# Attention with a group norm on one core: normalisation spread over steps, projections moved later, x loaded first, the last sums inverted from PSUM

## The chip, the cores and the metric

The kernel runs on one core of a Trainium2 chip. The metric is device time in microseconds (us) of one execution; the profile's span is the time from the first to the last instruction of one profiled execution. A core has five engines with a queue of instructions each: PE (matrix multiply; PEld is its weight load), DVE (vector), ACT (scalar, activation functions), POOL (GpSimd) and SP, which here only issues DMAs. PE writes to PSUM, a memory of eight banks; ACT and DVE copy from there to SBUF.

## The reference

```python
def reference(x, q_w, q_b, kv_w, kv_b):        # x: 32 images, 256 channels, 32 x 32 positions
    return x + attention(group_norm(x))

def group_norm(v, G=32, eps=1e-5):             # 32 groups of 8 channels, over 8 * 1024 values
    return (v - mean) / sqrt(var + eps)

def attention(xf):                             # S = 1024 positions, 8 heads of 32 channels
    q = q_w @ xf + q_b;  k, v = split(kv_w @ xf + kv_b)
    scores = q.T @ k / sqrt(32)
    scores = where(position of key < position of query, scores, -10000)
    attn = softmax(scores)
    attn = where(position of key < position of query, attn, 0)
    return attn @ v
```

All is float32. The first query sees no key, so its output is x alone.

## The kernel before

**Tiles and steps.** Channels lie on partitions, 256 channels are two groups `g` of 128, which are four heads each. The 1024 queries are two halves `hf` of 512 columns, the keys eight blocks `k` of 128. One *step* is one block of keys for four heads and one half of the queries. Since a query sees only earlier keys, half 0 has the blocks k = 0 to 2 and half 1 the blocks 0 to 6 (the fourth block of a half is done together with its second, in `blocks`), so an image has 2 x (3 + 7) = 20 steps (`N`): steps 0 to 2 are (g 0, half 0), 3 to 9 (g 0, half 1), 10 to 12 (g 1, half 0), 13 to 19 (g 1, half 1). With 32 images there are 640 steps.

**One step.** `scores` multiplies k by q into two PSUM tiles `sT` (tag sT has three buffers of two banks each), and ACT writes exp of each into the SBUF tile `e`. On the last blocks of a half POOL clears the entries of later keys (`affine_select`). Two steps later (`LAG = 2`) `values` multiplies `e` by v into `acc`, and DVE adds `e` to the running total. The total is no tile of its own: it is the `e` tile of the half's first block, k = 0, which has the tag `e0` and **two buffers**. The others have the tag `e` and four.

**The end of a half.** `values` of the last block ends with an ACT copy of `acc` to `num`. `sums` then lets PE add the total over partitions (`pd`, from `e` and the ones in `pick`), ACT copies `pd` to `den`, and a DMA writes it to DRAM. When an image's four halves are there, `gather` reads them back as 128 rows of 64, `invert` checks their range and takes the reciprocal on DVE (`inv`), and more DMAs bring the inverses back, spread over partitions, as `rb`. `finish` multiplies `num` by `rb`, adds the v bias and x, and stores it.

**Before an image's steps.** `load` brings x by DMA. `norm_channels` takes the statistics of each channel (DVE, `mv`), `norm_mean` averages them over a group on PE (`pm`), copies that with ACT (`mean`) and at once lets DVE work out `dev` from it; `norm_rstd` averages dev on PE (`pv`), adds eps on ACT and takes the power -0.5 on POOL; `norm_apply` writes `xn` on DVE. `projections` are 12 units of PE work: eight `project_qk` (`pp`) and four `project_v` (`ppv`), each ended by an ACT copy out of PSUM.

**PSUM.** sT takes six banks, acc one, and a single bank, the tag `misc`, serves pm, pv, pp, ppv and pd in turn: each has to be copied out before the next may start.

**Who sets the order.** PE, ACT, DVE and POOL run their instructions in the order in which the program is written (`manual_schedule`); SP's is chosen by the framework. The loop at the end goes over the steps: at step i it writes `scores` of step i, then the work that the table `at` has for i, then `values` of step i - 2, then what the table `after` has. Before the change, the statistics of image b + 2 stand at steps 4 and 5 of image b, mean at 8, rstd at 10, apply at 16 and 18; the projections of image b + 1 at 12 steps of image b; the sums of a half at the third step after its last (so at steps 5, 12, 15 and 2 of the next image). Images 0 and 1 are normalised and image 0 is projected ahead of the loop.

Of the kernel before, what the change touches and what calls it, by code (L numbers as in the profile page):

```python
# [9 lines left out]
F32 = mybir.dt.float32  # L10
# [7 lines left out]
P = 128  # L18
# [13 lines left out]
def tile_norm_attention_residual(  # L32
# [59 lines left out]


    wT = const.tile([P, NG, 3 * C], F32, name="wT")
    with tc.tile_pool(name="wload", bufs=3) as wload, tc.tile_pool(name="ps_w", bufs=2, space=PSUM) as ps_w:
        for n, w in enumerate((q_w, kv_w[0:C], kv_w[C : 2 * C])):
            wn = wload.tile([P, NG, C], F32, tag="wn", name=f"wn_{n}")
            nc.sync.dma_start(out=wn, in_=w.rearrange("(o p) c -> p o c", p=P))
            for cc in range(NG):
                pt = ps_w.tile([P, C], F32, tag="pt", name=f"wt_{n}_{cc}")  # L100
                for o in range(NG):
                    nc.tensor.transpose(pt[:, o * P : (o + 1) * P], wn[:, o, cc * P : (cc + 1) * P], ident)
                nc.vector.tensor_copy(wT[:, cc, n * C : (n + 1) * C], pt)
    qk_bias = const.tile([P, 2, NG], F32, name="qk_bias")
    nc.sync.dma_start(out=qk_bias[:, 0, :], in_=q_b.rearrange("(g p) -> p g", p=P))
    nc.sync.dma_start(out=qk_bias[:, 1, :], in_=kv_b[0:C].rearrange("(g p) -> p g", p=P))
    nc.vector.tensor_scalar_mul(qk_bias[:, 0, :], qk_bias[:, 0, :], SCALE)
    v_bias_col = const.tile([P, NG], F32, name="v_bias_col")
    nc.sync.dma_start(out=v_bias_col, in_=kv_b[C : 2 * C].rearrange("(g p) -> p g", p=P))
    v_bias = const.tile([P, C], F32, name="v_bias")  # L110
    nc.sync.dma_start(out=v_bias, in_=kv_b[C : 2 * C].rearrange("(o c) -> o c", o=1).broadcast_to([P, C]))

    def unshifted():
        xpool = tc.alloc_tile_pool(name="xpool", bufs=4)
        work = tc.alloc_tile_pool(name="work", bufs=2)
# [8 lines left out]
        live = {}  # L124
# [13 lines left out]

        def load(b):
            live["x", b] = xpool.tile([P, NG, S], F32, tag="x", name=f"x_{b}")  # L140
            nc.sync.dma_start(out=live["x", b], in_=x_in[b])
# [9 lines left out]
        def norm_mean(b):  # L151
# [4 lines left out]
            nc.scalar.copy(mean, pm[:, :NG])  # L156

# [4 lines left out]
            live["mean", b], live["dev", b] = mean, dev  # L162

        def norm_rstd(b):
            pv = misc(f"pv_{b}")
            product(pv[:, :NG], avg, live.pop(("dev", b)))
            rstd = small.tile([P, NG], F32, tag="rstd", name=f"rstd_{b}")
            nc.scalar.activation(rstd, pv[:, :NG], AF.Identity, bias=eps)
            nc.gpsimd.tensor_tensor(rstd, rstd, power, ALU.pow)
            live["rstd", b] = rstd  # L170

        def norm_apply(b, g):
            if g == 0:
                live["xn", b] = work.tile([P, NG, S], F32, tag="xn", name=f"xn_{b}")
            mean, rstd = live["mean", b], live["rstd", b]
            nc.vector.tensor_scalar(
                live["xn", b][:, g, :], live["x", b][:, g, :],
                mean[:, g : g + 1], rstd[:, g : g + 1], ALU.subtract, ALU.mult,
            )
# [100 lines left out]
        def sums(b, g, hf):  # L280
# [10 lines left out]
            nc.scalar.copy(den, pd)  # L291
            if n == 0:
# [6 lines left out]
        def gather(b):  # L299
# [243 lines left out]
```

## Time and profile before

| | |
|---|---|
| median of 3 runs | 2262.64 us (2260.61 to 2266.06) |
| the profiled execution's own time, and its span | 2263.33 us, 2261.6 us |
| PE busy | 2081.9 us, 92% of the span |
| DVE busy | 1514.2 us, 67% |
| ACT busy | 1492.0 us, 66% |
| POOL busy | 419.3 us, 19% |
| mean granted clock of PE, as a share of the full one | 0.970 |
| DMA | 108.01 MB, 48 GB/s in the mean |

Matmuls are pipelined, so that a row's duration overlaps the next row's by some 0.07 us or more; the time that one costs is best read from its start to the next start. An idle time in square brackets in a timeline is that of the engine ahead of the row, with what ended it.

### The profile page before, as it was taken

To read this page: it belongs to the slowest core of one execution; us is meant where nothing else is said; L and a number is where in the kernel's file an instruction comes from. 1 tells how busy PE (TensorE), PEld (TensorE's weight loads), DVE (VectorE), ACT (ScalarE), POOL (GpSimd) and SP (SyncE) were. 2 spreads that over 40 slices of the span, in tenths; PEclk is the share of its full clock that TensorE was granted. 3 is DMA by queue.
4 is the path that set the end of the run, shared out by engine and by line. 5 is a ranking of instruction groups with operands and counts; after the bars stand their busy time and mean duration, and the time that the engine had idled before them with its cause. 6 is when DMAs were issued, how large, how long until landed. Compare 5 with 4: busy or idle time off the path is not lost.

```text
span 2261.6 us, 50192 instructions
## 1 busy us (share of the span) xinstructions
PE 2081.9 (92%) x22030; PEld 733.3 (32%) x22030; DVE 1514.2 (67%) x1417; ACT 1492.0 (66%) x1985; POOL 419.3 (19%) x494
## 2 busy tenths in 40 slices
PE   4999999999999999999999999999999999999993
PEld 1333333333333333333333333333333333333331
DVE  2566767666767666776667676667676667766675
ACT  1767666667666676666676666676666766666773
POOL 0221121121121211211211212211212112112121
PEclk9999999999999999999999999999999999999997
DMA  2001111101111011111011111011110111110011
GB/s 91 2 31 50 50 48 59 56 24 59 43 55 59 31 50 58 41 58 59 30 51 49 49 59 50 30 59 43 55 59 34 46 56 42 58 59 31 31 40 59
DMA packets 47057, 108.01 MB, mean 48 GB/s; under 512 B 12656, under 2 KB 13552, under 8 KB 46832
## 3 DMA queue, kind: packets, MB, share of 16 engines
q1 hardware_dynamic: 46832, 104.74, 13.0%
q8 instruction: 174, 2.85, 0.5%
q14 instruction: 51, 0.42, 0.1%
HBM read 69.08 MB, written 35.65 MB: 46 GB/s over the span
## 4 chain that ended last, share of the span: by engine, by line
PE 73%; DVE 19%; ACT 4%; issue 3%; DMA 1%; POOL 1%; SPq 0%; DVEq 0%; POOLq 0%; ACTq 0%
PE sT L237 23%; PE pp L134 21%; PE acc L268 17%; DVE e L273 12%; PE ppv L134 6%; PE pd L286 6%; DVE rb L326 2%; ACT e L244 2%; DVE dev L159 1%; DVE rb L327 1%; DVE dev L160 1%; ACT num L277 1%; ACT q L193 1%; POOL e L250 1%; DMA rb<-inverses 0%
## 5 line engine op out<-in xcount | busy, mean ns | idle before, releaser
L273 DVE TENSOR_TENSOR e<-e,e 128x2048 f32<-128x2048 f32 (+3 forms) x640 | 1088.6, 1701 | 492.1 <-PE acc L268 192.0
L244 ACT ACTIVATE e<-sT 128x1024 f32<-128x1024 f32 (+1 forms) x1280 | 1127.8, 940 | 433.1 <-PE sT L237 424.9
L237 PE MATMUL sT<-q,k 32*128 32x512 f32 (+3 forms) x6144 | 721.2, 541 | 0.5 <-ACT e L244 0.5
L250 POOL TENSOR_SCALAR_AFFINE_SELECT e<-e 128x512 f32<-128x512 f32 (+1 forms) x384 | 351.0, 926 | 1781.9 <-ACT e L244 1042.2
L268 PE MATMUL acc<-e,v 128*32 128x512 f32 (+3 forms) x6144 | 617.4, 489 | 20.9 <-ACT num L277 11.7
L134 PE MATMUL pp<-xn,wT 128*32 128x512 f32 x4096 | 494.1, 600 | 5.9 <-ACT q L193 3.2
L237 PEld LDWEIGHTS sT<-q,k 32*128 32x128 f32 x6144 | 291.2, 187 | 433.8 <-issue 371.5
L268 PEld LDWEIGHTS acc<-e,v 128*32 128x32 f32 x6144 | 173.6, 110 | 349.5 <-issue 231.0
L134 PE MATMUL ppv<-wT,xn 128*32 128x256 f32 x4096 | 257.9, 394 | 10.9 <-ACT mean L156 8.0
L286 PE MATMUL pd<-e,pick 128*32 128x512 f32 x1024 | 150.1, 657 | 92.2 <-DVE e L273 92.2
L134 PEld LDWEIGHTS pp<-xn,wT 128*32 128x32 f32 x4096 | 107.0, 109 | 321.7 <-issue 234.8
L291 ACT COPY den<-pd 128x512 f32<-128x512 f32 x128 | 75.2, 588 | 184.4 <-PE pd L286 184.4
L134 PEld LDWEIGHTS ppv<-wT,xn 128*32 128x32 f32 x4096 | 122.9, 113 | 168.5 <-issue 68.8
L159 DVE TENSOR_TENSOR dev<-mv,mean 128x2 f32<-128x2 f32 x32 | 33.1, 1035 | 203.0 <-ACT mean L156 203.0
L326 DVE TENSOR_TENSOR rb<-num,rb 128x512 f32<-128x512 f32 x128 | 114.6, 896 | 9.8 <-DMA rb<-inverses 9.8
L193 ACT ACTIVATE k<-pp,qk_bias 128x512 f32<-128x512 f32 x128 | 88.1, 688 | 32.4 <-PE pp L134 32.4
L209 ACT COPY v<-ppv 128x512 f32<-128x512 f32 x128 | 75.1, 587 | 51.2 <-PE ppv L134 50.7
L327 DVE SCALAR_TENSOR_TENSOR rb<-rb,v_bias_col,x 128x512 f32<-128x512 f32 x128 | 105.4, 824 | 4.6
L193 ACT ACTIVATE q<-pp,qk_bias 128x512 f32<-128x512 f32 x128 | 88.1, 688 | 13.4 <-PE pp L134 9.8
L286 PEld LDWEIGHTS pd<-e,pick 128*32 128x32 f32 x1024 | 32.1, 112 | 176.6 <-DVE e L273 121.1
L148 DVE BATCH_NORM_STATS2 st<-x 128x6 f32<-128x512 f32 x128 | 80.1, 668 | 4.8 <-DMA x<-in_x_dram 4.8
L277 ACT COPY num<-acc 128x512 f32<-128x512 f32 x128 | 74.5, 582 | 3.7 <-PE acc L268 3.7
(39 smaller groups left out, 250.6 us busy)
## 6 DMA issues: line engine op xcount, KB each, us to landing
x<-in_x_dram SPq DMA_DIRECT2D x32, 1024.0 KB
rb<-inverses SPq DMA_DIRECT2D x128, 256.0 KB
out_dram<-rb SPq DMA_DIRECT2D x64, 512.0 KB
sums<-den SPq DMA_DIRECT2D x128, 8.0 KB
rows<-sums SPq DMA_DIRECT2D x32, 32.0 KB
inverses<-inv SPq DMA_DIRECT2D x32, 32.0 KB
wn<-in_L_conv_kv_w_dram SPq DMA_DIRECT2D x2, 256.0 KB
wn<-in_L_conv_q_w_dram SPq DMA_DIRECT2D x1, 256.0 KB
```

Source lines behind the costliest of these rows:

```text
L134: nc.tensor.matmul(out[part], lhsT=lhsT[:, part], rhs=rhs, start=start, stop=stop, skip_group_check=True)
L148: nc.vector.bn_stats(st[:, c, :], live["x", b][:, g, c * HALF : (c + 1) * HALF])
L193: nc.scalar.activation(live[key][:, cols], pp, AF.Identity, bias=qk_bias[:, n, g : g + 1], scale=(SCALE, 1.0)[n],)
L237: nc.tensor.matmul(pairs[j // 2][:, j % 2, cols], lhsT=kk[rows, kb * P : (kb + 1) * P], rhs=q[rows, hf * HALF + of.start : hf * HALF + of. ...
L244: nc.scalar.activation(e[:, 2 * a : 2 * a + 2, c0:], pairs[a][:, :, c0:], AF.Exp)
L250: nc.gpsimd.affine_select(out=diagonal, in_=diagonal, pattern=[[0, 4], [0, n], [1, P]], compare_op=ALU.is_gt, fill=0.0, base=0, channel_mu ...
L268: nc.tensor.matmul(acc[HD * j : HD * (j + 1), of], lhsT=live["v", b][:, kb, h * HD : (h + 1) * HD], rhs=e[:, j, cols], start=k == 0, stop= ...
L273: nc.vector.tensor_add(total[:, :, of], total[:, :, of], e[:, :, cols])
L277: nc.scalar.copy(live["num", b][:, g, hf * HALF : (hf + 1) * HALF], acc)
L286: nc.tensor.matmul(pd[HD * j : HD * (j + 1), :], lhsT=pick, rhs=total[:, j, :], start=True, stop=True, skip_group_check=True,)
L326: nc.vector.tensor_mul(rb[:, g, cols], num[:, g, cols], rb[:, g, cols])
L327: nc.vector.scalar_tensor_tensor(rb[:, g, cols], rb[:, g, cols], v_bias_col[:, g : g + 1], xt[:, g, cols], ALU.add, ALU.add)
```

## The change

Weights are loaded through ACT's queue, after the first two images' x, which now comes in two DMAs an image; ACT instead of DVE copies the transposed weights. The normalisation of an image is cut into eight functions, which stand at steps of their own: `dev` two steps after `mean`, `pv` eight steps after that, the power one step on and all of `xn` one more step on, in four pieces. The projections of an image stand from six steps before its first step to its step 11, ordered by the step that needs them; of image 0 two units are left ahead of the loop. The sums stand one step later (`SUMS = LAG + 2`), gather and invert at steps 4 and 6 of the next image, and `finish` stores each half by itself. The last image gathers three halves early, and its fourth is inverted by DVE directly from `pd` in two pieces. Nothing is added to or taken from what is computed.

```diff
+    def load_weights():
+            for wn, w in zip(wns, (q_w, kv_w[0:C], kv_w[C : 2 * C])):
+                nc.scalar.dma_start(out=wn, in_=w.rearrange("(o p) c -> p o c", p=P))
...
+                    nc.scalar.copy(wT[:, cc, n * C : (n + 1) * C], pt)
...
+        def load(b):
+            live["x", b] = xpool.tile([P, NG, S], F32, tag="x", name=f"x_{b}")
+            for g in range(NG):
+                nc.sync.dma_start(out=live["x", b][:, g, :], in_=x_in[b, :, g, :])
+
+        for b in range(min(2, B)):
+            load(b)
+        load_weights()
...
             nc.scalar.copy(mean, pm[:, :NG])
+            live["mean", b] = mean
+
+        def norm_deviation(b):
+            mv, mean = live["mv", b], live["mean", b]
...
-        def norm_rstd(b):
+            live["dev", b] = dev
+
+        def norm_variance(b):
             pv = misc(f"pv_{b}")
...
-            units = [lambda hf=hf, n=n: project_qk(b, 0, n, hf) for n in range(2) for hf in range(NH)]
-            units += [lambda n=n: project_v(b, n) for n in range(NB // 2)]
-            units += [lambda hf=hf, n=n: project_qk(b, 1, n, hf) for n in range(2) for hf in range(NH)]
-            return units
+            qk = [[lambda g=g, hf=hf, n=n: project_qk(b, g, n, hf) for n in range(2)] for g in range(NG) for hf in range(NH)]
+            v = [lambda n=n: project_v(b, n) for n in range(NB // 2)]
+            return qk[0] + v[:1] + qk[1] + v[1:3] + qk[2] + v[3:] + qk[3]
...
+        def finish_last(b):
+            g, hf = NG - 1, NH - 1
+            for c in range(2):
+                within = slice(c * HALF // 2, (c + 1) * HALF // 2)
+                nc.vector.reciprocal(
+                    live["rb", b][:, g, hf * HALF + within.start : hf * HALF + within.stop], live["pd", b][:, within]
+                )
+                finish(b, 3, within)
...
-                    when(b * N + s + LAG + 1, lambda b=b, g=g, hf=hf: sums(b, g, hf), after)
...
+        PROJECT = (-6, -5, -3, -2, -1, 1, 4, 5, 7, 8, 9, 11)
+        PREPARE = (-36, -35, -30, -28, -20, -19, -18, -18)
+        SUMS = LAG + 2
+        FINISH = (N + 11, N + 12, N + 14, N + 15)
```

**The sums on PE.** In the names, sT_1_1_0_2 is image 1, group 1, half 0, block 2, pd_1_1 the sums of image 1's second half, and the last number only counts tiles. PE's order at steps 11 to 13, before:

```order
L268 MATMUL acc_1_0_1_1073<-e_1_0_1_6_1175,v_1_550 32x256 x4
L237 MATMUL sT_1_1_0_2_0_1279<-q_1_1_773,k_1_1_848 128x256 x2
L237 MATMUL sT_1_1_0_2_1_1280<-q_1_1_773,k_1_1_848 128x256 x2
L268 MATMUL acc_1_1_0_1291<-e0_1_1_0_0_1208,v_1_550 32x512 x4
L286 MATMUL pd_1_1_1296<-e0_1_0_1_0_986,pick_67 32x512 x4
L237 MATMUL sT_1_1_1_0_0_1305<-q_1_1_773,k_1_1_848 128x512 x2
L237 MATMUL sT_1_1_1_0_1_1306<-q_1_1_773,k_1_1_848 128x512 x2
L134 MATMUL ppv_2_3_1313<-wT_77,xn_2_821 32x256 x16
```

and the same place now:

```order
L283 MATMUL acc_1_0_1_991<-e_1_0_1_6_1093,v_1_731 32x256 x4
L252 MATMUL sT_1_1_0_2_0_1181<-q_1_1_976,k_1_1_1040 128x256 x2
L252 MATMUL sT_1_1_0_2_1_1182<-q_1_1_976,k_1_1_1040 128x256 x2
L283 MATMUL acc_1_1_0_1197<-e0_1_1_0_0_1118,v_1_731 32x512 x4
L252 MATMUL sT_1_1_1_0_0_1203<-q_1_1_976,k_1_1_1040 128x512 x2
L252 MATMUL sT_1_1_1_0_1_1204<-q_1_1_976,k_1_1_1040 128x512 x2
L283 MATMUL acc_1_1_0_1197<-e_1_1_0_1_1146,v_1_731 32x384 x4
L283 MATMUL acc_1_1_0_1197<-e_1_1_0_1_1146,v_1_731 32x128 x4
L301 MATMUL pd_1_1_1221<-e0_1_0_1_0_899,pick_67 32x512 x4
L252 MATMUL sT_1_1_1_1_0_1230<-q_1_1_976,k_1_1_1040 128x512 x2
L252 MATMUL sT_1_1_1_1_1_1231<-q_1_1_976,k_1_1_1040 128x512 x2
L146 MATMUL pp_2_0_0_0_1243<-xn_2_889,wT_77 32x512 x8
```

The sums pd_1_1, which read the tile e0_1_0_1_0 of step 3, have moved from ahead of step 13's scores sT_1_1_1_0 to behind them.

**The exponentials on ACT.** ACT's order at steps 12 to 14, with the engines that each instruction waits for, before:

```order
L244 ACTIVATE e_1_1_0_2_1278<-sT_1_1_0_2_0_1279 128x2x256 [waits DVE_49,PE_49]
L244 ACTIVATE e_1_1_0_2_1278<-sT_1_1_0_2_1_1280 128x2x256 [waits PE_49]
L291 COPY den_1_1_1301<-pd_1_1_1296 128x512 [waits DMAHW6_49,PE_49]
L244 ACTIVATE e0_1_1_1_0_1304<-sT_1_1_1_0_0_1305 128x1024 [waits DVE_49,PE_49]
L244 ACTIVATE e0_1_1_1_0_1304<-sT_1_1_1_0_1_1306 128x1024 [waits PE_49]
L209 COPY v_2_1121<-ppv_2_3_1313 128x512 [waits PE_49]
```

and now:

```order
L259 ACTIVATE e_1_1_0_2_1180<-sT_1_1_0_2_0_1181 128x2x256 [waits DVE_49,PE_49]
L259 ACTIVATE e_1_1_0_2_1180<-sT_1_1_0_2_1_1182 128x2x256 [waits PE_49]
L259 ACTIVATE e0_1_1_1_0_1202<-sT_1_1_1_0_0_1203 128x1024 [waits DVE_49,PE_49]
L259 ACTIVATE e0_1_1_1_0_1202<-sT_1_1_1_0_1_1204 128x1024
L306 COPY den_1_1_1226<-pd_1_1_1221 128x512 [waits DMAHW2_49]
L259 ACTIVATE e_1_1_1_1_1229<-sT_1_1_1_1_0_1230 128x1024 [waits PE_49,Pool_49]
```

The copy of pd to den has moved behind the exponentials of step 13 and has lost its wait for PE, as has the second exponential: what they need of PE has already been waited for by the instruction ahead of them.

**The deviation on DVE.** DVE's order around `dev`, before (between two of the additions of a half 1):

```order
L273 TENSOR_TENSOR e0_2_0_1_0_1569<-e0_2_0_1_0_1569,e_2_0_1_2_1632 128x2048 [waits DVE_49,Activation_49]
L159 TENSOR_TENSOR dev_4_1749<-mv_4_1609,mean_4_1747 128x2 [waits Activation_49]
L160 TENSOR_TENSOR dev_4_1749<-dev_4_1749 128x2 [waits DVE_49]
L161 TENSOR_TENSOR dev_4_1749<-dev_4_1749,mv_4_1609 128x2 [waits DVE_49]
L273 TENSOR_TENSOR e0_2_0_1_0_1569<-e0_2_0_1_0_1569,e_2_0_1_3_1670 128x2048
```

and now:

```order
L288 TENSOR_TENSOR e0_1_0_1_0_899<-e0_1_0_1_0_899,e_1_0_1_6_1093 128x4x256 [waits Pool_49]
L346 TENSOR_TENSOR rb_0_1011<-num_0_389,rb_0_1011 128x512 [waits DMAHW6_49]
L347 SCALAR_TENSOR_TENSOR rb_0_1011<-rb_0_1011,v_bias_col_79,x_0_84 128x512 [waits DVE_49]
L171 TENSOR_TENSOR dev_3_1193<-mv_3_955,mean_3_1134 128x2 [waits Activation_49]
L172 TENSOR_TENSOR dev_3_1193<-dev_3_1193 128x2 [waits DVE_49]
L173 TENSOR_TENSOR dev_3_1193<-dev_3_1193,mv_3_955 128x2 [waits DVE_49]
```

The three operations of dev now stand behind the last addition of the half (block 6), and not between those of its blocks 2 and 3.

## Rows read from the trace of the kernel before

**Rows 1.** Who waited for whom: total us, times, longest.
```profile
DVE dev L159 <- ACT mean L156: 203.0, 32, 6.7
PE pd L286 <- DVE e L273: 92.2, 32, 3.4
```

**Rows 2.** Timeline of DVE at steps 8 to 11: start us, us, what.
```profile
975.35 1.09 DVE L159 TENSOR_TENSOR dev<-mv,mean 128x2 f32<-128x2 f32 x1 [6.74 <-ACT mean L156]
...
977.19 7.55 DVE L273 TENSOR_TENSOR e<-e,e 128x2048 f32<-128x2048 f32 x4
```

**Rows 3.** Timeline of PE at step 12 of two images: start us, us.
```profile
916.12 1.07 PE L268 MATMUL acc<-e,v 128*32 128x512 f32 x8 [0.21 <-POOL rstd L169]
920.19 1.71 PE L286 MATMUL pd<-e,pick 128*32 128x512 f32 x8 [3.00 <-DVE e L273]
921.84 2.09 PE L237 MATMUL sT<-q,k 32*128 32x512 f32 x8
...
984.63 1.06 PE L268 MATMUL acc<-e,v 128*32 128x512 f32 x8 [0.21 <-POOL rstd L169]
```

**Rows 4.** Busy time by stretch: PE, PEld, DVE, ACT, POOL, PEclk, DMA, GB/s.
```profile
920.00:922.00 2.00, 1.81 (x12) 0.32 (x12) 1.96 (x4) 0.05 (x1) 0.00 (x0) 0.62 0.00 0
922.00:924.00 2.00, 2.00 (x12) 0.50 (x16) 1.97 (x3) 0.58 (x2) 0.00 (x0) 0.53 0.67 266
...
2228.00:2232.00 4.00, 1.50 (x24) 0.64 (x24) 3.59 (x3) 0.59 (x1) 0.87 (x2) 1.00 0.00 0
```

**Rows 5.** Timeline at steps 15 and 16, sums without a wait: start us, us.
```profile
862.50 1.06 PE L268 MATMUL acc<-e,v 128*32 128x512 f32 x8
862.66 1.94 ACT L244 ACTIVATE e<-sT 128x1024 f32<-128x1024 f32 x2 [0.36 <-PE sT L237]
...
863.38 1.04 PE L286 MATMUL pd<-e,pick 128*32 128x512 f32 x8
...
864.36 1.14 PE L237 MATMUL sT<-q,k 32*128 32x512 f32 x8
864.49 0.59 ACT L291 COPY den<-pd 128x512 f32<-128x512 f32 x1
...
865.43 1.92 PE L134 MATMUL pp<-xn,wT 128*32 128x512 f32 x16
```

**Rows 6.** Timeline from the start to the first scores: start us, us.
```profile
8.99 2.29 SPq L141 DMA_DIRECT2D x<-in_x_dram  x4
14.18 1.29 DVE L148 BATCH_NORM_STATS2 st<-x 128x6 f32<-128x512 f32 x2 [4.76 <-DMA x<-in_x_dram]
...
19.98 1.53 DVE L176 TENSOR_SCALAR xn<-x,mean,rstd 128x1024 f32<-128x1024 f32 x2 [1.64 <-POOL rstd L169]
...
26.38 3.50 PE L134 MATMUL pp<-xn,wT 128*32 128x512 f32 x16 [0.37 <-ACT rstd L168]
...
29.95 0.69 ACT L193 ACTIVATE q<-pp,qk_bias 128x512 f32<-128x512 f32 x1 [3.63 <-PE pp L134]
30.69 1.92 PE L134 MATMUL pp<-xn,wT 128*32 128x512 f32 x16 [0.82 <-ACT q L193]
...
59.49 1.77 PE L237 MATMUL sT<-q,k 32*128 32x512 f32 x12
```

**Rows 7.** Timeline of the last half image: start us, us.
```profile
2200.31 1.14 PE L237 MATMUL sT<-q,k 32*128 32x512 f32 x8
...
2232.59 1.06 PE L286 MATMUL pd<-e,pick 128*32 128x512 f32 x8 [2.79 <-DVE e L273]
...
2237.97 0.22 DVE L305 SCALAR_TENSOR_TENSOR in_range<-rows,in_range 128x64 f32<-128x64 f32 x1 [5.43 <-DMA rows<-sums]
...
2238.37 0.54 DVE L308 RECIPROCAL inv<-rows 128x64 f32<-128x64 f32 x1
...
2245.20 0.69 DVE L326 TENSOR_TENSOR rb<-num,rb 128x512 f32<-128x512 f32 x1 [6.29 <-DMA rb<-inverses]
...
2254.25 0.75 DVE L327 SCALAR_TENSOR_TENSOR rb<-rb,v_bias_col,x 128x512 f32<-128x512 f32 x1
```

More of the change, by code (lines that the diff above doesn't have):

```diff
@@ L94, in tile_norm_attention_residual @@
     wT = const.tile([P, NG, 3 * C], F32, name="wT")
[L95 to L103, printed above, removed]
@@ L309, in invert @@
             live["inv", b] = dram.tile([4, 4, HALF], F32, tag="inv", name=f"inverses_{b}")
-            nc.sync.dma_start(out=spread_rows(live["inv", b]), in_=inv)
-        def spread(b):
-            rb = work.tile([P, NG, S], F32, tag="rb", name=f"rb_{b}")
-            for n in range(4):
+            nc.sync.dma_start(out=spread_rows(live["inv", b])[part], in_=inv[part])
+            live["rb", b] = work.tile([P, NG, S], F32, tag="rb", name=f"rb_{b}")
+            for n in ns:
                 g, hf = divmod(n, NH)
@@ L368, in unshifted @@
         with tc.manual_schedule(engines={ENG.PE, ENG.Activation, ENG.DVE, ENG.Pool}):
-            for b in range(min(2, B)):
-                load(b)
-                for f in prepare(b):
-                    f()
-            for f in projections(0):
-                f()
-            for i in range(max(max(at), len(steps) + LAG) + 1):
+            prepare(0, [None] * 8)
+            for n, f in zip((None, None, 0, 0, 1, 1) + PROJECT[6:], projections(0)):
+                if n is None:
+                    f()
+                else:
+                    when(n, f)
@@ new lines, in unshifted @@
+            if B > 1:
+                prepare(1, (None, None, 2, 4, 6, 7, 8, 9))
+            for b in range(B):
+                first, last = b * N, b == B - 1
+                if b >= 1:
+                    for n, f in zip(PROJECT, projections(b)):
+                        when(first + n, f)
+                if b >= 2:
+                    when(max(first - 2 * N - 2, 0), lambda b=b: load(b))
+                    prepare(b, [first + n for n in PREPARE])
+                for s, (g, hf, k) in enumerate(per):
+                    if k == hf * BPH + 2:
+                        n = first + s + (LAG if last and s == N - 1 else SUMS)
+                        when(n, lambda b=b, g=g, hf=hf: sums(b, g, hf), after)
+                if not last:
+                    when(first + N + 4, lambda b=b: gather(b, every))
+                    when(first + N + 6, lambda b=b: check_sums(b, every))
+                    when(first + N + 6, lambda b=b: invert(b, every))
+                    for n in every:
+                        when(first + FINISH[n], lambda b=b, n=n: finish(b, n))
+                else:
+                    when(first + N - 4, lambda b=b: gather(b, every[:3]), after)
+                    when(first + N - 2, lambda b=b: check_sums(b, every[:3]))
+                    when(first + N - 2, lambda b=b: invert(b, every[:3]))
+                    for n in every[:3]:
+                        when(first + N + n - 1, lambda b=b, n=n: finish(b, n))
+                    when(first + N + LAG, lambda b=b: gather(b, every[3:]))
+                    when(first + N + LAG, lambda b=b: finish_last(b))
+                    when(first + N + LAG, lambda b=b: check_sums(b, every[3:]))
@@ L376, in unshifted @@
+            for i in range(max(max(at), max(after), len(steps) + LAG) + 1):
                 if i < len(steps):
```

104 lines of the change are left out of this document (52 added, 52 removed).

## The prediction

> **What bounds the kernel now.** The granted clock and the busy shares come first: PE is busy 92% of the span, no other engine over 67%, and PE's clock averages 0.970. So the place to look is PE's remaining idle time, and the list of waits names it: 92.2 us of PE waiting for DVE ahead of `pd`, 32 times [rows 1]. The list has 203.0 us of DVE waiting for ACT's `mean` as well [rows 1], which alone would cost nothing, since DVE has time to spare; what ties the two together is the order. On DVE's timeline at steps 8 to 11 the reader sees `dev` wait 6.74 us for the mean, and behind it four additions of 7.55 us in one piece that had been ready meanwhile [rows 2]. DVE comes to the end of the half late, and `pd` needs the half's last addition.
>
> The price is in PE's timeline. At step 12 `pd` starts 4.07 us behind the start of `acc` (916.12 to 920.19) [rows 3]; where nothing holds it, it is 0.88 us (862.50 to 863.38) [rows 5]. That is 3.19 us of waiting. After it PE runs slowly: `pd` takes 1.65 us to the next start against 0.98, and the scores 2.09 against 1.14 [rows 3, 5], 1.62 us in all. The stretch shows why: the granted clock is 0.62 and then 0.53 just there [rows 4], so 1.2 GHz instead of 2.4 for some 2 us. An image lasts 68.51 us (916.12 to 984.63) [rows 3], 4.81 of them this stall. Of the 92.2 us [rows 1], 30 times 3.0 are 90, so it happens in the 30 images 1 to 30 alike.
>
> **What goes.** `dev` now stands behind the half's last addition, two steps after `mean`, and the sums one step later. Ahead of the addition that `pd` needs, DVE then has only `finish` of one half at step 11. It reaches that addition some 4 us before PE reaches `pd`, worked out from steps of 1.7 to 3.8 us. I take the whole 4.81 us as gone. The copy of the mean, the power and the smaller waits (0.21 us at each step 12 [rows 3]) stay as they are or trade places.
>
> **What comes in its stead.** The moved sums collide with a buffer. The total of a half is the `e0` tile of its first block, of which there are two. The total of step 3 is freed by `pd` of step 13, but step 13's own exponentials write the same buffer. Before, that `pd` stood ahead of the step's scores; now it stands behind them, and ACT's first exponential has to wait for it (the order shows it by the copy of `pd`, which needs no wait for PE any more). At step 3 of each image it is the same with the last half of the image before. At steps 0 and 10 the buffer has been free for four steps.
>
> The price, from the end of `pd`: the exponentials start 0.07 us later, take 1.83 us together up to the next ACT row (862.66 to 864.49), then the copy `den` takes 0.59 us, and PE goes on 0.05 us after such a copy [rows 5, 6]. That is 2.54 us to the next projection, which needs the bank `misc` empty. Without the wait PE would be there after the next scores, 1.07 us (864.36 to 865.43) [rows 5]. PE thus loses 1.47 us, twice an image, 2.94 us. This wait isn't in the trace of before, so it has bounds: nothing, if the buffer is free after all (a rival below), and about 2.0 us if the next scores, whose second tile waits for the first exponential to empty a PSUM buffer, run half of their 1.07 us late. I take 1.47: that second tile can start as soon as one of the two exponentials is through, about a microsecond before it is missed. What ACT has lost it regains in the next three steps, where it has some 3 us of work in steps of 3.4 to 3.8.
>
> An image then takes 68.51 - 4.81 + 2.94 = 66.64 us, 1.87 less; 30 of them give **-56.1 us**.
>
> **The start.** Before, SP issues x behind the weights at 8.99, the statistics begin at 14.18, `xn` at 19.98, the first projection at 26.38 behind the second image's normalisation, and the first scores at 59.49 [rows 6]. Now x is issued at about 1 us; with its 5.2 us to landing (8.99 to 14.18) the statistics begin at about 6, `xn` some 5.8 us later (14.18 to 19.98) and the first projection at 12.3. That one takes 3.50 us at the slow clock, its copy 0.69, the second 1.92 and a copy again [rows 6], so the scores start at about 19.3: -40.2. But only two of image 0's twelve units are ahead of the loop now. The other ten are PE work in the loop, 1.75 us each (a 1.92 us row with its overlap taken off): +17.5. Crowded into steps 0 to 6 they wait for one another's copies: +3, an estimate from the 0.82 us that such a pair costs [rows 6]. The new wait at one place each in images 0 and 31, 2.94, less the half of the 2.2 us that are left of `pd`'s waits for these two images [rows 1]: +1.8. Together **-17.9 us**. The weights on ACT's queue hold ACT for seven issues, but it has nothing else to do before x is there.
>
> **The end.** From step 10 of the last image to the end it is 61.3 us now (2200.31 to 2261.6) [rows 7]. In the changed order the third sums end after some 20.1 us, since ACT alone sets the pace of steps without projections. The rows come back 4.3 us after `pd` (2233.65 to 2237.97), range check and reciprocal take 0.94, and the first `rb` is there 6.3 us after that (2238.91 to 2245.20) [rows 7]. DVE stands at `finish` for it, with three additions behind; those and three `finish` take 11.1 us, `pd` 1.1. Then two reciprocals of 256 columns: 0.54 us for 64 [rows 7] gives 2.2 each if it grows with the columns, 0.54 if it doesn't; I take 2.2, since the range check of the same 64 columns takes only 0.22 [rows 7]. With multiply and add it is 5.9 us, then 0.6 for the last check and 6.6 to the end, as before (2255.0 to 2261.6) [rows 7]. That is 56.9: **-4.4 us**, between -10 and +4.
>
> **Edits at no cost.** Two DMAs more for x and two more stores an image lie on SP, which mostly waits; x is loaded at step 18 and used six steps on, some 20 us against its 5.2 to land [rows 6]. Should that cover go, DVE would stand at the statistics with the next additions behind it. `xn` in four pieces and the power at another step lie in DVE's and POOL's spare time, with the projections that need `xn` twelve steps later.
>
> **The sum.** -56.1 - 17.9 - 4.4 = -78.4 us on the profiled execution's 2263.33 gives 2184.9; the median of the runs is 0.7 below that execution, so **2184 us**.
>
> **The rivals.**
> A. *The buffer costs nothing.* If the exponentials of steps 3 and 13 needn't wait, the 62 waits of 1.47 us fall away: 2184 - 91 = 2093. For it: ACT has a third of its time free. Against it: the copy's lost wait in the order.
> B. *The clock falls at the new waits*, the rival on the other side. Twice an image PE is idle in two pieces, 0.5 and 0.9 us, around half of the scores. If the clock fell each time as it does at step 12 [rows 4], 1.62 us a time would be 100 us for 62: 2284, slower than now. It decides from 1.26 us a time (78.4 over 62). Against it: in the last half image PE was busy for 1.50 of 4 us with the clock at 1.00, and the `pd` after an idle 2.79 us ran at full speed in 1.06 [rows 4, 7]; and between the projections of the start, 0.82 us idle after each 1.92, the next ones kept their 1.92 [rows 6]. The Trainium skill speaks for it: "TensorE: Matmul & The Clock Gate", section "A second HAM failure mode: psum-queue depth-cycling", tells of a kernel in which short idle times between groups of matmuls, by the cycling of PSUM buffers, sufficed to let the clock swing between its two levels. By that page the sum would be the 2284 of this rival, by the rows the 2184 of the forecast; I go by the rows.
> C. *The sums stay late.* If DVE still came to the half's last addition as late as now, the 4.81 us would stay and the new wait would come on top, as ACT would stand as well: 2263 - 22 + 30 x 2.94 = 2329. For it: `finish` can be stretched beside POOL's work. Against it: DVE gains the 6.74 us that it now stands idle at `dev` [rows 2].
>
> **How the numbers follow.** Forecast 0.76, A 0.10, B 0.09, C 0.05. The forecast's own bounds: the new wait at 2.0 us adds 62 x 0.53 = 33 us, start and end some 8 more: 2225. At half its price it is 46 less, start and end 10 less: 2128. A part of A reaches into that, and little more than 2 in 10 lie outside 2122 to 2225. About 0.2% (4.5 us) is what a measurement of this kernel can tell from no change. Faster by more: the forecast and A, 0.86; slower: B and a part of C, 0.11; the same: a C of which half is true, 0.03.
>
> **What would show it.** In the changed kernel's profile: the wait of DVE for the mean gone and that of PE's `pd` for DVE under 0.5 us an image; ACT's `e` waiting for `pd` twice an image, and PE's `pp` and `ppv` behind `den` by 1 to 2 us; an image in 66.6 us; the clock at 1.00 throughout; the first scores near 19 us; DVE waiting for `rb` once in the last image and two reciprocals of 2.2 us at the end. I am wrong if ACT's exponentials of steps 3 and 13 start 1.2 us behind their scores as the others do, if the clock is below 0.97, or if `pd` still waits for DVE.

## The result, and the profile after

| | before | after |
|---|---|---|
| median | 2261.67 us (4 runs) | 2167.33 us (4 runs, 2167.05 to 2167.56) |
| ratio, 95% interval | | 0.9579 [0.9563, 0.9596] |
| profiled execution, span | 2263.33, 2261.6 us | 2167.23, 2165.3 us |
| PE busy, mean granted clock | 92%, 0.970 | 96%, 0.994 |
| DVE, ACT, POOL busy | 67%, 66%, 19% | 68%, 69%, 21% |

The change makes the kernel 4.2% faster, 94 us; the forecast was 2184 us, 78 less than before. The list of waits of the changed kernel (who waits for whom: total us, times, longest) shows both halves of the argument:

```profile
ACT e L259 <- PE pd L301: 200.8, 63, 3.2
PE pd L301 <- DVE e L288: 12.9, 1, 12.9
DVE dev L171 <- ACT mean L164: 2.9, 1, 2.9
```

The two waits of [rows 1] are gone: DVE's for the mean is 2.9 us instead of 203.0, and `pd` waits for DVE once only, in the last half of the last image. In their place stands the wait that the order foretold, ACT's exponentials for `pd`, 63 times.

PE's timeline at step 12 of image 0 and at steps 12 to 14 of image 13 (start us, us, instruction, idle time ahead of it in brackets) answers to [rows 3]:

```profile
65.67 1.07 PE L283 MATMUL acc<-e,v 128*32 128x512 f32 x8 [0.30 <-ACT num L292]
...
924.89 1.06 PE L283 MATMUL acc<-e,v 128*32 128x512 f32 x8 [0.30 <-ACT num L292]
925.89 1.14 PE L252 MATMUL sT<-q,k 32*128 32x512 f32 x8
926.96 1.07 PE L283 MATMUL acc<-e,v 128*32 128x384 f32 x16
927.85 1.04 PE L301 MATMUL pd<-e,pick 128*32 128x512 f32 x8
928.82 2.34 PE L252 MATMUL sT<-q,k 32*128 32x512 f32 x8
931.42 1.92 PE L146 MATMUL pp<-xn,wT 128*32 128x512 f32 x16 [0.27 <-ACT den L306]
```

and ACT's at the same place:

```profile
924.64 1.10 ACT L259 ACTIVATE e<-sT 128x512 f32<-128x512 f32 x2
928.96 1.94 ACT L259 ACTIVATE e<-sT 128x1024 f32<-128x1024 f32 x2 [3.22 <-PE pd L301]
930.78 0.59 ACT L306 COPY den<-pd 128x512 f32<-128x512 f32 x1
```

`pd` starts 0.89 us behind `acc` and runs at full speed. ACT stands idle for 3.22 us although the scores of step 13 have been there since 927, and starts when `pd` ends. From the scores of step 14 to the projection it takes 2.60 us (928.82 to 931.42) instead of 1.07. An image lasts 66.09 us (924.89 less 65.67, over 13 images), 2.42 less than before. The row of 2.34 us for the scores isn't a slow PE, it contains the wait for ACT to empty a PSUM tile: in that stretch the granted clock is 1.00 (columns as in [rows 4]):

```profile
926.00:928.00 2.00, 2.00 (x28) 0.84 (x32) 1.91 (x1) 0.00 (x0) 0.48 (x1) 1.00 0.03 8
928.00:930.00 2.00, 1.95 (x16) 0.30 (x4) 1.93 (x4) 1.04 (x2) 0.00 (x0) 1.00 0.00 0
930.00:932.00 2.00, 1.70 (x12) 0.58 (x16) 1.97 (x4) 2.00 (x3) 0.00 (x0) 1.00 0.35 131
```

At the start, POOL's and PE's rows answer to [rows 6]:

```profile
9.96 0.22 POOL L108 TENSOR_SCALAR qk_bias<-qk_bias 128x2 f32<-128x2 f32 x1 [7.88 <-DMA qk_bias<-in_L_conv_q_b_dram]
10.14 0.40 POOL L83 TENSOR_SCALAR_AFFINE_SELECT avg<-avg 128x128 f32<-128x128 f32 x1
```
```profile
10.60 0.29 PE L146 MATMUL pm<-mv,avg 128*32 128x2 f32 x8 [4.08 <-POOL avg L83]
...
14.06 3.64 PE L146 MATMUL pp<-xn,wT 128*32 128x512 f32 x16 [0.86 <-DVE xn L191]
...
21.29 1.14 PE L252 MATMUL sT<-q,k 32*128 32x512 f32 x8 [0.81 <-ACT k L208]
```

The first scores start at 21.29 instead of 59.49, 2 us later than forecast: the scaling of the q bias, now on POOL, waits for its DMA, and the second half of `avg`, which PE needs for the first mean, is queued behind it. At the end, the last rows answer to [rows 7]:

```profile
2107.98 1.14 PE L252 MATMUL sT<-q,k 32*128 32x512 f32 x8
...
2150.08 1.93 PE L301 MATMUL pd<-e,pick 128*32 128x512 f32 x8 [12.95 <-DVE e L288]
...
2152.70 1.76 DVE L359 RECIPROCAL rb<-pd 128x256 f32<-128x256 f32 x1 [2.67 <-ACT den L306]
```

From step 10 of the last image to the end it is 57.3 us (2107.98 to 2165.3), 61.3 before.

**Where the 96.3 us of the two spans lie.** Up to step 10 of the last image the changed kernel is 92.3 us ahead (2200.31 against 2107.98). Thirty images of 2.42 us (68.51 - 66.09) are 72.6 of them, the other 19.7 are what the forecast calls the start, and 4.0 come from the end. These 19.7 don't lie at the start alone. In the kernel before, `acc` of step 12 starts as follows in images 0 and 31:

```profile
96.44 1.06 PE L268 MATMUL acc<-e,v 128*32 128x512 f32 x8 [0.21 <-POOL rstd L169]
...
2207.12 1.07 PE L268 MATMUL acc<-e,v 128*32 128x512 f32 x8 [0.78 <-ACT num L277]
```

At step 12 of image 0 the changed kernel is 30.8 us ahead (96.44 against 65.67), at step 12 of image 30 103.2 (2151.67 against 2048.50), and at step 12 of image 31 only 92.5 (2207.12 against 2114.59). The last image thus pays 10.7 us back: seven of its projections, which the kernel before had done in the image ahead of it, now stand in its own steps (some 1.75 us each, 12 in all, of which a part falls into time that PE had idle; no run shows this by itself).

### The profile page after: what moved, and what is told of

Same layout as the page of the kernel before. It is cut to its first block, busy times and chain, and to the rows that moved or that the text cites. A ratio compares the mean times of both kernels' runs of the same rounds, so it can differ in the third digit from the quotient of the medians.

```text
span 2165.3 us, 50543 instructions
## 1 busy us (share of the span) xinstructions
PE 2084.0 (96%) x22030; PEld 730.1 (34%) x22030; DVE 1478.1 (68%) x1480; ACT 1493.4 (69%) x1991; POOL 449.4 (21%) x495
## 4 chain that ended last, share of the span: by engine, by line
PE 80%; ACT 9%; issue 6%; POOL 3%; DMA 1%; DVE 1%; ACTq 0%; POOLq 0%; SPq 0%; DVEq 0%
PE sT L252 23%; PE pp L146 22%; PE acc L283 22%; PE ppv L146 8%; PE pd L301 5%; ACT e L259 5%; POOL e L265 2%; ACT den L306 2%; ACT num L292 1%; ACT k L208 1%; DMA qk_bias<-in_L_conv_q_b_dram 0%; PE pm L146 0%; DVE e L288 0%; DMA rb<-inverses 0%; DVE rb L359 0%
## 5 line engine op out<-in xcount | busy, mean ns | idle before, releaser
L265 POOL TENSOR_SCALAR_AFFINE_SELECT e<-e 128x512 f32<-128x512 f32 (+1 forms) x384 | 420.1, 1094 | 1672.4 <-ACT e L259 1562.0
L252 PE MATMUL sT<-q,k 32*128 32x512 f32 (+3 forms) x6144 | 754.3, 525 | 6.2 <-ACT k L208 0.8
L146 PE MATMUL pp<-xn,wT 128*32 128x512 f32 x4096 | 494.2, 600 | 10.7 <-ACT den L306 8.3
L146 PE MATMUL ppv<-wT,xn 128*32 128x256 f32 x4096 | 247.6, 382 | 9.1 <-ACT den L306 8.3
L191 DVE TENSOR_SCALAR xn<-x,mean,rstd 128x512 f32<-128x512 f32 x128 | 73.0, 630 | 175.1 <-POOL rstd L184 175.1
L301 PE MATMUL pd<-e,pick 128*32 128x512 f32 x1024 | 134.2, 596 | 14.1 <-DVE e L288 12.9
L346 DVE TENSOR_TENSOR rb<-num,rb 128x512 f32<-128x512 f32 x129 | 87.6, 679 | 5.1 <-DMA rb<-inverses 5.0
L306 ACT COPY den<-pd 128x512 f32<-128x512 f32 x128 | 75.5, 590 | 15.5 <-PE pd L301 15.5
L224 ACT COPY v<-ppv 128x512 f32<-128x512 f32 x128 | 75.0, 586 | 10.7 <-PE ppv L146 8.5
```

The source lines that it names most:

```text
L146: nc.tensor.matmul(out[part], lhsT=lhsT[:, part], rhs=rhs, start=start, stop=stop, skip_group_check=True)
L252: nc.tensor.matmul(pairs[j // 2][:, j % 2, cols], lhsT=kk[rows, kb * P : (kb + 1) * P], rhs=q[rows, hf * HALF + of.start : hf * HALF + of. ...
L265: nc.gpsimd.affine_select(out=diagonal, in_=diagonal, pattern=[[0, 4], [0, n], [1, P]], compare_op=ALU.is_gt, fill=0.0, base=0, channel_mu ...
L301: nc.tensor.matmul(pd[HD * j : HD * (j + 1), :], lhsT=pick, rhs=total[:, j, :], start=True, stop=True, skip_group_check=True,)
L346: nc.vector.tensor_mul(rb[:, g, cols], num[:, g, cols], rb[:, g, cols])
```

## The experiments

The medians of the kernel before beside these runs were 2263.8 to 2264.4 us, so times of different groups of runs can be compared within some 3 us.

**1. A third buffer for the totals.** It takes away what the exponentials wait for, and the order of the instructions stays.

```diff
-            e = epool.tile([P, 4, HALF], F32, tag=tag, bufs=2 if k == 0 else None, ...)
+            e = epool.tile([P, 4, HALF], F32, tag=tag, bufs=3 if k == 0 else None, ...)
```

> The changed kernel, with a third buffer for the totals (tag e0), nothing else. Theory: the exponentials of steps 3 and 13 wait for pd only because of the buffer, and each of the 63 waits costs PE 1.53 us (2.60 us from the scores to the next projection instead of 1.07). They go: ACT's wait for pd falls from 200.8 us to nearly nothing, an image takes 66.09 - 3.06 = 63.0 us, and the time is 2167 - 63 x 1.53 = 2071 us (2060 to 2085). Rival: PE would lose the time elsewhere (ACT, which does not get its work done sooner, or the bank misc, becomes the limit in the same steps): 2140 to 2167.

Measured: 2069.95 us (2069.57 to 2070.5), ratio to the kernel before 0.9143 [0.9128, 0.9158]. ACT's wait for `pd` is no longer in the list. PE at the same steps:

```profile
889.04 1.14 PE L252 MATMUL sT<-q,k 32*128 32x512 f32 x8
890.11 1.92 PE L146 MATMUL pp<-xn,wT 128*32 128x512 f32 x16
```

From the scores to the projection it is 1.07 us again, and an image lasts 63.03 (885.11 to 948.14). The new wait therefore cost 97 us, as much as the whole change brought, and one more buffer gives all of it back: the rival, in which PE loses the time elsewhere, falls.

**2. The sums back at their old step.** All four, and then only those of the two halves 1.

```diff
-        SUMS = LAG + 2
+        SUMS = LAG + 1
```

> The changed kernel with the sums one step earlier, where they stood before (LAG + 1). Theory: DVE now finishes the last addition of a half some 4 us before pd needs it, so pd waits for nothing there, and the exponentials of steps 3 and 13 find their buffer free: -3.06 us an image. But at steps 5 and 15 the new table has a projection in the same step, so pd has to wait until ACT has copied the projection out of the bank misc: 0.7 us of copy and up to 1 us of ACT's other work, twice an image, +1 to +3 us. 2075 to 2165, I take 2110. Rival (the sums were moved because DVE is late): pd waits for DVE again, 3 us with the slow clock behind it, an image back at 68 us or more, 2200 or more.

```diff
-                        n = first + s + (LAG if last and s == N - 1 else SUMS)
+                        n = first + s + (LAG if last and s == N - 1 else SUMS - hf)
```

> The changed kernel, with two buffers for the totals as it has, and only the sums of the two halves 1 one step earlier (steps 12 and 22, where no projection stands); those of the halves 0 stay at steps 6 and 16. Theory: the first of these two sums frees the buffer ahead of the scores of steps 13 and 3, so the new wait goes as it does with a third buffer, and no sums share their step with a projection, so the 1.1 us an image that the sums one step earlier for all four halves cost aren't there either: an image 63.0 us, the time within 5 us of the kernel with three buffers, 2070 (2065 to 2080). Rival (the third buffer gives ACT or DVE more room than the one wait shows): 2085 to 2167.

Measured: 2102.69 us (ratio 0.9292 [0.9276, 0.9307]) and 2081.21 us (0.9199 [0.9184, 0.9214]). The first is within its range, the second 1.2 us above its own (2065 to 2080) and 11 above the 2070 that I took. Both are free of the new wait without a third buffer, and in neither does `pd` wait for DVE before the last half of the last image, so DVE is in time for the old step too: moving the sums was not needed to take away the stall. But both are slower than the third buffer, and not for the reason that I gave. PE's rows with all four sums moved back, at step 15:

```profile
908.37 1.92 PE L146 MATMUL pp<-xn,wT 128*32 128x512 f32 x16
910.11 1.04 PE L283 MATMUL acc<-e,v 128*32 128x512 f32 x8
911.10 1.07 PE L301 MATMUL pd<-e,pick 128*32 128x512 f32 x8
912.10 1.14 PE L252 MATMUL sT<-q,k 32*128 32x512 f32 x8
913.17 1.07 PE L283 MATMUL acc<-e,v 128*32 128x512 f32 x8
914.16 1.36 PE L252 MATMUL sT<-q,k 32*128 32x512 f32 x8
915.46 1.93 PE L146 MATMUL ppv<-wT,xn 128*32 128x256 f32 x32
```

`pd` follows the projection of its own step 0.99 us behind `acc` instead of 0.88, so the bank `misc` costs 0.1 us and not the 1 or 2 that I expected. What costs are steps 3, 6, 13 and 16, which now have neither projection nor sums. At step 16 only one `acc` stands between its scores (912.10) and those of step 17 (914.16), and these take 1.30 us to the next start instead of 1.07. I read it as a wait for ACT to empty their PSUM tile, since the row is longer and the granted clock is 1.00 from 906 to 918 us; no run tests this reading. Added up over an image, from start to start, the scores take 21.38 us against 20.60 with the third buffer, `acc` 0.24 and `pd` 0.08 us more: 64.12 against 63.03. With the mixed sums two such places are left, steps 3 and 13, of 0.17 us each, and an image takes 63.36. One step later, the sums fill the steps that have no projection; so placed, and with the buffer that this needs, the kernel is the fastest of the three.

**3. dev back at the step of mean,** the rest of the change as it is.

```diff
-        PREPARE = (-36, -35, -30, -28, -20, -19, -18, -18)
+        PREPARE = (-36, -35, -30, -30, -20, -19, -18, -18)
```

> The changed kernel with dev back at the step of mean, ahead of the additions, so that DVE waits for mean again; the rest of the change stands. Theory: the wait of DVE comes back (some 3 to 6 us a time, 30 times), and with it some of the lateness of the last addition of the half, but the sums one step later give it 2 us of cover: pd waits 0 to 2 us, the time is 2167 to 2230, I take 2185. Rival (the spread normalisation alone took the stall away): pd waits its 3 us again and the clock falls behind it, 2290 or more. Other rival (the later sums alone took it away): 2167, no wait of pd.

Measured: 2195.24 us, ratio 0.9696 [0.968, 0.9712], 28 us more than the changed kernel. DVE and PE at the end of the half:

```profile
869.19 0.68 DVE L171 TENSOR_TENSOR dev<-mv,mean 128x2 f32<-128x2 f32 x1 [6.91 <-ACT mean L164]
...
875.22 1.22 DVE L288 TENSOR_TENSOR e<-e,e 128x1024 f32<-128x1024 f32 x1
```
```profile
874.67 1.07 PE L283 MATMUL acc<-e,v 128*32 128x384 f32 x16
876.49 1.06 PE L301 MATMUL pd<-e,pick 128*32 128x512 f32 x8 [0.75 <-DVE e L288]
877.49 2.34 PE L252 MATMUL sT<-q,k 32*128 32x512 f32 x8
```

DVE waits its 6.91 us as before the change, the half's last addition ends at 876.4, and `pd`, one step later now, waits 0.75 us for it instead of 3.00. So the wait at `dev` is what makes `pd` late, and the later sums cover most of it. After 0.75 us the clock doesn't fall: `pd` takes 1.00 us to the next start, and the granted clock is 1.00 from 872 to 880 us.

**4. The kernel before with the deviation later,** and with it what has to follow it. `dev` is a function of its own here, the fourth in the list. Twice: with `pv` four steps later and one projection moved out of its way, and with `pv` and the power eight steps later, at a step without a projection, and `xn` behind them.

```diff
-                for n, f in zip((4, 5, 8, 10, 16, 18), prepare(b + 2)):
+                for n, f in zip((4, 5, 8, 12, 14, 16, 18), prepare(b + 2)):
...
-                for n, f in zip((1, 3, 4, 6, 7, 9, 11, 13, 14, 16, 17, 19), projections(b + 1)):
+                for n, f in zip((1, 3, 4, 6, 7, 9, 11, 13, 16, 17, 18, 19), projections(b + 1)):
```

> The kernel before, with dev moved from step 8 to step 12, the average of dev (pv) from step 10 to 14, and for its sake one projection from step 14 to 18; sums, projections, start and end as before. Theory: DVE no longer stands at dev with four additions behind it, pd of step 12 waits for nothing, the clock stays up, and since the sums stand where they did there is no new wait either: 4.81 to 5.5 us less an image, 2262 - 30 x 5 = 2112 (2095 to 2130), less than the changed kernel has without its start and end. Rival: finish of the image before, which stands among the same additions, keeps DVE late, pd still waits 1 us or more: 2180 to 2250.

```diff
-                for n, f in zip((4, 5, 8, 10, 16, 18), prepare(b + 2)):
+                for n, f in zip((4, 5, 8, 12, 18, 19, 19), prepare(b + 2)):
```

> The kernel before, with dev moved from step 8 to 12, pv and the power from step 10 to 18 (where no projection stands), and xn from steps 16 and 18 to 19. No projection is moved, unlike in the earlier run with dev at 12, in which steps 13 to 15 had one projection less and PE waited there for ACT's exponentials (scores of 2.15 us to the next start where 1.07 is usual). Theory: with the stall gone and no such gap an image takes 68.51 less 4.81 to 5.5, 63.0 to 63.7 us, and the time is 2100 to 2118, 2108 at the likeliest. Rival (something else of the old order costs that 1 us, as the copy of acc that PE waits for): 2145 to 2155 again.

Measured: 2152.0 us (ratio 0.95 [0.9484, 0.9516]) and 2149.24 us (0.9495 [0.948, 0.951]). Both are faster than the whole change, with the start and the end of the kernel before. The stall is gone, but an image takes 64.68 and 64.70 us, 3.8 less than before and not 5: my expectation missed by 1.2 us an image, some 40 us in all, twice. The second time is in the rival's range, 2145 to 2155. In the first kernel its own edit costs time, in the second `pd` waits a little for DVE again:

```profile
882.44 0.24 PE L134 MATMUL pv<-dev,avg 128*32 128x2 f32 x8
882.52 0.62 PE L271 MATMUL acc<-e,v 128*32 128x256 f32 x8
883.07 1.74 PE L240 MATMUL sT<-q,k 32*128 32x512 f32 x8
885.22 1.07 PE L271 MATMUL acc<-e,v 128*32 128x512 f32 x8 [0.41 <-ACT num L280]
```
```profile
893.91 0.82 PE L240 MATMUL sT<-q,k 32*128 32x256 f32 x8
895.10 1.92 PE L134 MATMUL pp<-xn,wT 128*32 128x512 f32 x16 [0.36 <-ACT rstd L171]
...
904.43 1.06 PE L271 MATMUL acc<-e,v 128*32 128x512 f32 x8 [0.30 <-ACT num L280]
905.85 1.06 PE L289 MATMUL pd<-e,pick 128*32 128x512 f32 x8 [0.35 <-DVE e L276]
```

In the first, step 14 has `pv` in place of a projection, and the scores behind it take 2.15 us to the next start. In the second, `pv` is followed by scores of 256 columns and a projection, which waits for the copy `rstd`: 1.19 us instead of the 0.65 of experiment 1 (0.82 in the kernel before); `pd` of step 2 waits for DVE, since `xn` stands late (1.42 us from `acc` to `pd` instead of 0.86). I read from these rows that a step with only two columns of `pv` or `pm` in place of a projection has too little work for PE. My rival, something else of the old order, holds as far as that; but the copy of `acc` that it named isn't it, since its waits (0.30 and 0.21 us) are those of the kernel of experiment 1 as well.

**5. The start.** The kernel before with x loaded first and the weights through ACT's queue (an image's x still in one DMA), and the changed kernel with all of image 0's projections ahead of the loop. Of the first only the new order of the loads is shown:

```diff
+        for b in range(min(2, B)):
+            load(b)
+        load_weights()
```

> The kernel before, with only the loads changed: x of the first two images ahead of the weights, weights through ACT's queue, their copies on ACT, the scaling of the bias on POOL. All projections and the normalisation of images 0 and 1 stay ahead of the loop. Theory: the statistics begin some 9 us earlier (4.9 instead of 14.18) but the average over groups waits for the second affine_select of avg behind the bias (10.6 as in the changed kernel), so the first projection starts not 9 but some 8 to 10 us earlier, and the first scores as much: 2262 - 9 = 2253 (2250 to 2257). What is left of the 20 us that the start brought comes from the projections that moved into the loop. Rival (the start is bound by the chain of projections, which wait for the weights): 2260 to 2264.

```diff
-            for n, f in zip((None, None, 0, 0, 1, 1) + PROJECT[6:], projections(0)):
+            for n, f in zip((None,) * 12, projections(0)):
```

> The changed kernel with all twelve projections of image 0 ahead of the loop, as before the change, and everything else changed. Theory: what the start gains beyond the loads comes from these ten units, which take 2.7 us each when they wait for one another's copies and 1.75 in the loop, among the scores: +10 x 0.95 = 9.5 us, 2174 to 2180, at the likeliest 2177, with the first scores at 48 us. Rival (in the first steps of the loop they wait for their copies as much, so that it makes no difference where they stand): 2165 to 2170.

Measured: 2262.15 us, ratio 0.9992 [0.9983, 1.0002], and 2183.45 us, ratio 0.9647 [0.9632, 0.9662]. With x first, the first scores start at 54.49 us, 5.0 earlier than before [rows 6] and half of what I expected. The time lies in the rival's range, and the runs can't tell it from no change. The rival's cause, the weights, isn't it: the first projection still stands behind the normalisation of image 1 and starts 0.66 us after that image's `pv` (20.53 to 21.19). In the profiled execution 4.9 us of the lead are there at step 12 of image 0 and 4.4 in image 31. With all projections ahead, the first scores start at 47.09 and the time is 16.1 us more than the changed kernel's instead of 9.5. By step 12 of image 0 it is 10.4 us behind (76.06 against 65.67), about as expected; at step 13 comes a stall that I hadn't foreseen:

```profile
81.79 1.92 PE L301 MATMUL pd<-e,pick 128*32 128x512 f32 x8 [2.15 <-DVE e L288]
83.64 3.28 PE L252 MATMUL sT<-q,k 32*128 32x512 f32 x8
86.85 2.81 PE L146 MATMUL pp<-xn,wT 128*32 128x512 f32 x16
```
```profile
78.00:80.00 2.00, 1.64 (x22) 0.42 (x16) 1.97 (x2) 0.00 (x0) 1.85 (x1) 1.00 0.00 0
...
82.00:84.00 2.00, 2.00 (x10) 0.36 (x4) 1.93 (x4) 0.24 (x1) 0.00 (x0) 0.50 0.00 0
...
86.00:88.00 2.00, 2.00 (x12) 0.40 (x12) 0.00 (x0) 2.00 (x3) 0.00 (x0) 0.50 0.05 12
```

PE, with fewer projections to do, is early, DVE late (image 1's `xn` stands among its additions, 68.80 to 74.55 us), and `pd` waits 2.15 us; behind it the granted clock is 0.50 (1.2 GHz) until 88 us, and the projection takes 2.63 us to the next start instead of 1.74. By step 2 of image 1 the gap is 15.5 us (114.20 against 98.67).

**6. The end.** The last fourth of the sums over DRAM, as the others.

```diff
-                    when(first + N + LAG, lambda b=b: finish_last(b))
                     when(first + N + LAG, lambda b=b: check_sums(b, every[3:]))
+                    when(first + N + LAG, lambda b=b: invert(b, every[3:]))
+                    when(first + N + LAG, lambda b=b: finish(b, 3))
```

> The changed kernel, with the sums of the last half of the last image read back by DMA, inverted as rows and spread by DMA again, as the other three, in place of two reciprocals from PSUM. Theory: the reciprocals from PSUM took 1.76 us each where the rows take 0.54, but the way over DRAM has two transfers of 4.3 and 6.3 us: about 2.1 for the write's issue and the den copy less 3.5, so 6 to 9 us more, 2173 to 2177. Rival (the two transfers and a single multiply-add are no slower than two long reciprocals): within 2 us of 2167.

Measured: 2175.99 us, ratio 0.9612 [0.9596, 0.9628], 8.7 more than the changed kernel. DVE waits 5.99 us for the rows and 6.50 us for `rb`, which outweighs the 3.5 us of the two reciprocals from PSUM.

**7. The bias out of the way.** First with the mixed sums, then with the third buffer.

```diff
-            nc.gpsimd.tensor_scalar_mul(qk_bias[:, 0, :], qk_bias[:, 0, :], SCALE)
...
             prepare(0, [None] * 8)
+            nc.vector.tensor_scalar_mul(qk_bias[:, 0, :], qk_bias[:, 0, :], SCALE)
```

> The kernel with the sums mixed (halves 1 one step earlier), and the scaling of the q bias moved from POOL, where it stood ahead of the second affine_select of avg and waited for its DMA until 9.96 us, to DVE behind image 0's xn. Theory: the average pm starts when the second group's statistics are done (8.3 us instead of 10.6), the first scores 2 to 2.5 us earlier than the 21.3 of the changed kernel, the end as much earlier: 2 us below the kernel with the sums mixed, about 2068. Rival (the first projection then waits for the weights' copies instead): no difference.

> The changed kernel with a third buffer for the totals and the scaling of the q bias on DVE behind image 0's xn. Theory: the two gains are at different places and add up: 2069.95 less the 2 to 3 us that the bias gave with the sums mixed (its first scores came at 19.16 instead of 21.29): 2067. Rival (the scores that start earlier only wait for the projections of the first steps): 2070.

Measured: 2078.18 us (ratio 0.9187 [0.9172, 0.9202]) and 2067.70 us (0.9139 [0.9126, 0.9151]), 3.0 and 2.3 us less than without. The 2.3 are between two groups of runs, and so less than the medians alone can tell; the rows bear them out: the first mean is taken at 8.54 instead of 10.60, `pd` is 2.0 to 2.1 us earlier than in experiment 1 in each of the 32 images, and the first scores start where the prediction had put them:

```profile
8.54 0.28 PE L145 MATMUL pm<-mv,avg 128*32 128x2 f32 x8 [1.90 <-DVE mv L156]
...
19.32 1.14 PE L251 MATMUL sT<-q,k 32*128 32x512 f32 x8 [0.81 <-ACT k L207]
```

This last kernel has the lowest time of all, 8.6% less than the kernel before and 4.6% less than the changed one (2067.70 over 2167.33).

## Why the prediction was right

The forecast was 2184, the time 2167. Its steps, one by one:

- **What goes, 4.81 us an image.** Right in place and cause: experiment 3 brings the wait back with `dev` alone, experiment 4 takes the stall away with `dev` and what follows it. The last addition ends at 921.12 and `pd` follows at 927.85, so DVE is 6.7 us early; I had said 4. The count is one too high: the stall is in images 1 to 29. Image 30, in whose steps no later image is normalised, has none (2151.67 from `acc` to 2152.53 for `pd`), and in image 0 `pd` waits 1.14 us. That the sum doesn't show it is luck: in images 7, 14 and 24 the clock stayed low for longer, and from step 12 to step 12 they took 69.9 us. Mis-sized is the sentence that the smaller waits stay or trade places. Summed from start to start over an image, before and after, `acc` falls by 3.12 us and `pd` by 0.71 (the stall, and `pd` at half speed). The scores rise by 1.40: 3.07 more for the two new waits, 0.95 less for the slow row behind the stall, and 0.7 less elsewhere, 0.6 of it behind the steps 8 and 18, which had no projection (there the scores of 256 columns took 1.08 and 0.82 us to the next start, the wait for the mean included, and now 0.64 and 0.65). These 0.7 us an image, some 20 in all, are what the forecast lacks.
- **The new wait, 1.47 us a place.** It is 1.53 (2.60 - 1.07), and the time comes back in full when the buffer is there (97.4 us for 63 places, 1.55 each). The upper bound of 2.0 and rival A, the free buffer, are refuted. The places are 63 and not 62: the last image has two, at steps 3 and 13. The sum over 30 images is -72.6 us instead of -56.1: 20 more from the smaller waits, less 4 since the new one takes 3.07 us an image and not 2.94.
- **The start, -17.9.** -19.7: the 30.8 us of image 0 less the 10.7 that the last image pays back, to within 0.4 us. That the number is so near is in part luck, since two terms were off in opposite directions: the first scores came 2.0 us later than 19.3 (the bias on POOL, experiment 7), and the ten units in the loop cost 5.1 less than 17.5 + 3. Ahead of the loop they take 25.8 us (21.29 to 47.09), and by step 12 of image 0 the kernel that has them there is only 10.4 behind; so they cost 15.4 in the loop, 1.5 each. The other way round, moving them into the loop gains 10.4 us by that step; the loads alone bring 5.0 up to the first scores (experiment 5).
- **The end, -4.4.** -4.0. The reciprocals of 256 columns take 1.76 us, not 2.2, but the first starts late: `pd` runs at half speed after PE's 12.95 us without work (1.93 us instead of 1.04, at a granted clock of 0.50), and the first reciprocal starts 2.62 us after `pd` instead of 1.1, as the copy of `pd` to `den` ends.
- **Rival B, the clock at the new waits.** Refuted: the granted clock is 1.00 in every stretch around steps 12 to 15, and `pd` keeps its 1.04. The Trainium skill's page "TensorE: Matmul & The Clock Gate", section "A second HAM failure mode: psum-queue depth-cycling", tells of a kernel in which idle times between groups of matmuls, by the cycling of PSUM buffers, came often enough to let the clock swing. In this case's trace they come twice in an image of 66.09 us, and there the clock didn't fall; a kernel in which they come more often wasn't run.
- **Rival C, the sums stay late.** Refuted by `pd`'s one wait for DVE.

What I didn't weigh is how the gain splits. Moving the three tiny operations of `dev`, with what follows them, is worth 112 us by itself (experiment 4), more than everything together, while the later sums, with two buffers, bring a wait of 97 us that a third buffer takes away. The second kernel of experiment 4 needs 1.67 us an image more than the 63.03 of experiment 1 (64.70), and the rows give all of it: 0.54 at `pv`, 0.44 at `pm` (1.09 instead of 0.65), 0.56 by the wait of `pd`, 0.13 in the scores of steps 1 and 11. What stays open is how the loads, the projections and the normalisation of image 1, which moved into the loop as well and which no run moves alone, share the start's 19.7 us to better than a few us: the second kernel of experiment 5 has a stall of its own in it.

## What to carry to other kernels

When an operation is moved behind another on one engine, list the buffers that it frees, and who writes them next: here the wait moved from a reader (`pd`) to the next writer (the exponentials) and cost as much as the change gained, and one buffer more was all that was needed. When the engine that bounds a kernel waits for one with time to spare, look for the operation at which the latter stands idle earlier with work queued behind it; here it was enough to move that one, and nothing had to become faster. Count, too, in how many images a wait really stands, and don't multiply one image's by all of them. And try the smallest part of a change alone before keeping the whole of it.

## What the runs showed of the hardware

- **Not every wait of PE costs clock.** The granted clock stayed at 1.00 with PE idle for 0.75 us ahead of `pd` (experiment 3) and through the new waits, and fell to 0.50 to 0.62 after idle times of 2.15 us (experiment 5) and 3.00 us [rows 3, 4]. What follows can cost more than the wait itself: in experiment 5 the gap to the changed kernel grew by 5.1 us from step 12 to step 2 of the next image, 2.15 of them the wait.
- **The length of the wait alone doesn't decide it.** After 2.79 us in the last half of the kernel before, `pd` still ran in 1.06 us [rows 7], at a granted clock of 1.00 from 2226 to 2234 us. And behind the same 3.00 us the clock fell at different moments: in image 12 `pd` itself was slow [rows 3], in image 8 it took 1.00 us to the next start, and the scores behind it 1.80 and the projection 2.67 instead of 1.07 and 1.75.

```profile
646.13 1.06 PE L286 MATMUL pd<-e,pick 128*32 128x512 f32 x8 [3.00 <-DVE e L273]
647.13 1.87 PE L237 MATMUL sT<-q,k 32*128 32x512 f32 x8
648.93 2.84 PE L134 MATMUL ppv<-wT,xn 128*32 128x256 f32 x32
```

- **A reciprocal on DVE takes longer with more columns.** It took 0.54 us for 64 columns from SBUF and 1.76 for 256 from PSUM, 3.3 times as long for four times the columns; no run separates the columns from the memory that it reads.
- **A wait of a queue that is idle for most of the time** can be on the path: POOL is 21% busy, and a scaling of 0.22 us, which waited 7.88 us for its DMA, held up the first scores by 2.0 us (21.29 against 19.32).
